# Moving the deep neighbour lists and the biases behind the first blocks of attention in a sparse graph-attention kernel

## The chip, the cores and the metric

The kernel runs on one NeuronCore of a Trainium2 chip. The metric is the time on the device in microseconds (us), lower is better. Five engines work from queues of their own: TensorE (PE, matrix products), VectorE (DVE), ScalarE (ACT), GpSimd (POOL) and SyncE (SP). POOL issues the indirect transfers (gathers and scatters by a list of rows), SP and ACT the plain ones.

## The reference

One layer of graph attention with a residual and a layer norm. There are 16 graphs (b) of 1024 nodes with 512 features in 8 heads of 64, and one adjacency matrix of zeros and ones, shared by all graphs.

```python
q = (x @ Wq + bq).reshape(b, n, H, HD)
k = (x @ Wk + bk).reshape(b, n, H, HD)
v = (x @ Wv + bv).reshape(b, n, H, HD)
scores = einsum('bqhd,bkhd->bhqk', q, k) / sqrt(HD)
scores = scores + (1.0 - adj) * -1e9
out = einsum('bhqk,bkhd->bqhd', softmax(scores), v).reshape(b, n, d)
return layernorm(x + out @ Wo + bo)
```

The entries of adj are drawn with a probability of about 1/256 for the pair on average, weighted so that the first nodes have many neighbours and the last ones few. All is float32.

## The kernel before, in words

Since a node has few neighbours, the kernel gathers keys instead of multiplying all pairs. It ranks the nodes by their number of neighbours, once, and cuts the ranked nodes into 8 tiles of 128. In tile t each node has `OWN[t]` blocks in which one row holds one neighbour of one query (`OWN = (2, 1, 2, 3, 4, 5, 5, 7)`). Tiles 6 and 7 have nodes with more neighbours; what is left over is packed into 1 and 5 further blocks (`BLOCKS`), in which a row holds some query and some key. These need the *deep lists*: which rows, and for which query. `edges(t)` makes them, for t = 7 with up to 80 neighbours and for t = 6 with up to 16.

A *place* is a step of the main loop, numbered n. Places 0 to 543 are the blocks of attention, 34 for each graph (tile 1 is left out, since its queries have one key at most). At place n several blocks are in work at different stages: the gather of keys and values of block n + 8 (`gather`, L984, POOL; 128 rows of 1024 numbers), `products` and `scores` of block n + 4 (qk at L1005 and s at L1009, DVE), the exponential of n + 3 and the weighing of n + 2 (L1019 and L1029, ACT), the sum over a tile's blocks (L1045 on DVE, or for deep blocks L1054 and L1055 on PE). A finished tile is transposed (poT, L1088) and multiplied with Wo (po, L639).

The *fronts* are PE's other work: for each graph the transposes of x (pxT, L606), the products with Wq (pq, L639), and a seven-product scheme for Wk and Wv on a pair of tiles (pair(b, j) takes tiles 2j and 2j+1): products x, pp and z at L763, with PSUM results p6, p7 and p4 in a ring of four buffers named fill (`fill_psum`), and x and z in a bank of their own. DVE and ACT combine them: e (L776), w (L779), g (L782), kv (L786, L791, L795), four sums of x before (L623 to L626), vsum (L701, L704) over the values. When all of a graph's keys and values are written to memory, the mean of its values is made (pm L708, copy L712, written by SP at L713), and `set_up[b]` lets the gathers of that graph start.

The order on each engine is the order in which this loop issues the instructions, and it is written out by hand. `later(k, fn)` puts an action k places on. PE's units are dealt out by credit: each place gets a share of PE time, and units are taken while credit is above 0. The costs are the constants `PRODUCT = 0.86`, `SUM = 0.87`, `TRANSPOSE = 0.44`. Ahead of place 0 lies the lead-in, places -LEAD_IN to -1, with fronts alone: a share of LEAD_SHARE = 3.3 up to place FRONT_BY, then START_SHARE = 2.0. In the first graph's 34 places the share is

```python
goal = fronts_time - (n // NBT + 2 + ahead / NBT) * batch_time
share = (max(0.0, left - goal) + kept * NPAIR * PRODUCT + NS * SUM) / NBT
```

so fronts that the lead-in left over are made up in these places.

Beside the units run generators, each advanced by one `yield` a place: `loads` (weights and biases), `ranks` (the ranking), `checks`, `edges(7)` and `edges(6)`, started at the places in `REST_FROM`, and `bias_setup`, started at `BIAS_AT`. In `edges` the row of adj is gathered (codes, L494), multiplied by the place numbers (L499), and the largest entries are taken out eight at a time, by a maximum (L518) and a removal (L520). For t = 7, sixteen candidates of every 64 columns are taken first (L511 to L513, into found), and ten maxima with nine removals then run on the 256 candidates. From the counts (est, L531) a product over the rows gives each list's start (poff, L534), DVE makes a mask from it (of, L546 and L547), and PE's products (pe, L557) and transposes (pof, L578) turn it into the rows to gather (key_row, L571; query_row, L572) and the sums' matrix. `bias_setup` makes the norm of bk (L351 to L353), columns of the biases (pb, L356 to L363) and bo + bv Wo (pb of L367, L369).

Work buffers come from rings by tag: kvg (8), kv (5), y (6), o (2), pv0 (3), and a new tile waits until the tile that had its buffer is done with.

Of the kernel before, what the change touches and what calls it, by code (L numbers as in the profile page):

```python
# [10 lines left out]
F32 = mybir.dt.float32  # L11
# [6 lines left out]
HEADS = 8  # L18
# [13 lines left out]
KG_BUFS, Q_BUFS, QT_BUFS, PV_BUFS, Y_BUFS = 8, 5, 3, 5, 6  # L32
# [13 lines left out]
EARLY = 13  # L46

FIRST = 11
LEAD_IN = 39
FRONT_BY = -14  # L50
SEGMENT = 64
TOP = 8
ADJ_AT = {-36: (0,), -35: (1, 2), -34: (3, 4), -33: (5,), -32: (6, 7)}
CHECKS_AT = -27
BIAS_AT = -8
REST_FROM = {7: -24, 6: -9}

PRODUCT = 0.86
SUM = 0.87
# [6 lines left out]
P = 128  # L66
# [103 lines left out]
def kernel(  # L170
# [37 lines left out]
    B, N, D = x.shape  # L208
    HD = D // HEADS
    NPAIR = D // P  # L210
# [29 lines left out]
    def broadcast(t, v):  # L240
        nc.scalar.dma_start(t, bass.AP(tensor=v.tensor, offset=v.offset, ap=[[0, P], [1, D]]))
# [4 lines left out]
    with ExitStack() as main:  # L246
        one = main.enter_context(tc.tile_pool(name="one", bufs=1))
        work = main.enter_context(tc.tile_pool(name="work", bufs=1))
# [4 lines left out]
        def fill_psum(name):  # L253
            return psum.tile([P, HALF], F32, tag="fill", name=name, bufs=4)
# [52 lines left out]
        residual = {i: dram.tile([P, D], F32, name=f"residual_{i}") for i in sorted(STORED)}  # L307
        zeros = work.tile([P, D + HEADS], F32, tag="pv0", name="zeros", bufs=3)
        nc.gpsimd.memset(zeros, 0.0)
        bias_rows = work.tile([2 * NPAIR, D + HEADS], F32, tag="pv0", name="bias_rows", bufs=3)[:, 0:P]  # L310
        bv_rows = work.tile([NPAIR, D + HEADS], F32, tag="pv0", name="bv_rows", bufs=3)[:, 0:P]

        def loads():

# [31 lines left out]
        def bias_setup():  # L346
            bk_bc = work.tile([P, D], F32, tag="y", name="bk_bc", bufs=Y_BUFS)
            broadcast(bk_bc, bk)
            yield
            n4 = small.tile([P, NPAIR], F32, name="bk_norms", bufs=1)  # L350
            nc.vector.tensor_tensor(bk_bc, bk_bc, bk_bc, op=OP.mult)  # L351
            nc.vector.tensor_reduce(n4, bk_bc.rearrange("p (h d) -> p h d", d=P), axis=AX.X, op=OP.add)
            nc.vector.tensor_reduce(bk_norm, n4, axis=AX.X, op=OP.max)  # L353
            yield
            pb = fill_psum("pb")
            nc.tensor.transpose(pb[:, 0:2 * NPAIR], bias_rows, ident[:2 * NPAIR, :2 * NPAIR])  # L356
            nc.tensor.transpose(pb[:, 2 * NPAIR:3 * NPAIR], bv_rows, ident[:NPAIR, :NPAIR])
            yield
            nc.vector.tensor_copy(bias_qk, pb[:, 0:2 * NPAIR])
            bv_col = one.tile([P, NPAIR], F32, name="bv_col")  # L360
            nc.vector.tensor_copy(bv_col, pb[:, 2 * NPAIR:3 * NPAIR])
            bvb = work.tile([P, NPAIR, P], F32, tag="y", name="bvb", bufs=Y_BUFS)
            nc.vector.tensor_copy(bvb, bv_col[:, :, None].to_broadcast([P, NPAIR, P]))  # L363
            yield
            pb = fill_psum("pb3")
            for c in range(NPAIR):
                nc.tensor.matmul(pb, bvb[:, c, :], W["o"][:, c, :], start=(c == 0), stop=(c == NPAIR - 1))  # L367
            yield
            nc.vector.tensor_tensor(bo_bc, pb, bo_bc, op=OP.add)  # L369
# [18 lines left out]
        now, plan, rest, urgent, known, waiting, combined = [0], {}, {}, [], [], [], []  # L388
# [9 lines left out]
        def most(t, scratch, copied):  # L398
            nc.vector.tensor_tensor(scratch, ADJ[t], place, op=OP.mult)
            nc.vector.max(out=asked[:, t, 2:], in_=scratch)  # L400
            nc.scalar.activation(copied, ADJ[t], AF.Copy, accum_out=asked[:, t, 1:2])

        def ranks():
# [6 lines left out]
            keys, row = (work.tile([P, N], F32, tag="kv", name=name, bufs=5) for name in ("keys", "key_of"))  # L410
            while now[0] <= max(ADJ_AT):
                for t in ADJ_AT.get(now[0], ()):
                    most(t, keys, row)
# [64 lines left out]
        def checks():  # L478
            for t in range(NT):

                a = ADJ[t]
                nc.scalar.activation(a, a, AF.Square, bias=neg_one, scale=2.0)
                nc.scalar.activation(a, a, AF.Square, bias=neg_one, accum_out=check[:, t:t + 1])
                yield
# [5 lines left out]
        def edges(t):  # L490
            nb, J, K = BLOCKS[t], DEGREE[t], OWN[t]
            tag, bufs = ("kvg", KG_BUFS) if J > 16 else ("kv", 5)
            v = work.tile([P, N], F32, tag=tag, name=f"codes_{t}", bufs=bufs)
# [3 lines left out]
            for _ in range(3):  # L497
                yield
            nc.vector.tensor_tensor(v, v, place, op=OP.mult)  # L499
            of = v[:, 0:nb * P]  # L500
            st = small.tile([P, 4], F32, name="est")
            deg, end, lim, off = (st[:, i:i + 1] for i in range(4))
            kl = small.tile([P, J + 3], F32, tag=f"kl{J}", name=f"kl_{t}", bufs=1)
# [1 line left out]
            if J > SEGMENT:  # L505

                assert J <= N // SEGMENT * 16 <= D
                found = work.tile([P, D], F32, tag="o", name=f"found_{t}", bufs=2)[:, 0:N // SEGMENT * 16]
                for i in range(N // SEGMENT):
                    piece, top = v[:, ts(i, SEGMENT)], found[:, ts(i, 16)]  # L510
                    nc.vector.max(out=top[:, 0:8], in_=piece)  # L511
                    nc.vector.scalar_tensor_tensor(piece, piece, top[:, 7:8], piece, op0=OP.is_lt, op1=OP.mult)
                    nc.vector.max(out=top[:, 8:16], in_=piece)  # L513
                    if i % 4 == 3:
                        yield
                v = found
            for r in range(J // 8):
                nc.vector.max(out=kl[:, ts(r, 8)], in_=v)  # L518
                if r < J // 8 - 1:
                    nc.vector.scalar_tensor_tensor(  # L520
                        v, v, kl[:, r * 8 + 7:r * 8 + 8], v, op0=OP.is_lt, op1=OP.mult
                    )
                    if J <= SEGMENT or r % 3 == 2:
                        yield
            if J > SEGMENT:
# [4 lines left out]

            nc.vector.tensor_scalar(deg, ranked[:, t, 1:2], -float(K), 0.0, op0=OP.add, op1=OP.max)  # L531
            yield
            po = fill_psum(f"poff_{t}")
            nc.tensor.matmul(po[:, 0:1], before, deg, start=True, stop=True)  # L534
            yield
# [6 lines left out]
            nc.vector.scalar_tensor_tensor(  # L542
                check[:, NT + t:NT + t + 1], deg, float(K - J), lim, op0=OP.add, op1=OP.max
            )
            o, span = of, place[:, 0:nb * P]
            nc.vector.tensor_scalar(o, span, off, None, op0=OP.is_gt)  # L546
            nc.vector.scalar_tensor_tensor(o, span, end, o, op0=OP.is_le, op1=OP.mult)  # L547
            yield
            step = min(nb, HALF // (J + 3))
            assert step * J <= D  # L550
# [39 lines left out]
        def load_x(b, t):  # L590
            if b < B:
                if b and not known:
                    waiting.append((b, t))
                    return
                X[b, t] = work.tile([P, D], F32, tag="x", name=f"x_{b}_{t}", bufs=3)
                if b:
                    gather_x(X[b, t], b, t)
                else:
                    nc.sync.dma_start(X[b, t], x[b, ds(t * P, P), :])
# [571 lines left out]
        prep = {}  # L1171
        for t, n in REST_FROM.items():
            prep.setdefault(n, []).append(edges(t))
        prep.setdefault(BIAS_AT, []).append(bias_setup())
        prep.setdefault(CHECKS_AT, []).append(checks())
        preps = [loads(), ranks()]
        prep.setdefault((B - 1) * NBT, []).append(guard())
        prep.setdefault(NBT, []).append(bias_pieces())
        with tc.manual_schedule():
# [6 lines left out]
            batch_time = fronts_time / B  # L1186
            finishing, last_finish, reloads, last_reload = [], -LEAD_IN, 0, 0
            fronts_end = (B - 1) * NBT - 12
            credit = 0.0
            for t in range(3):  # L1190
                load_x(0, t)
            n = -LEAD_IN
            while n < total or plan or rest or urgent or done or finishing or spilled or not guarded:
                now[0] = n
                if n < 0:
                    share = START_SHARE if n > FRONT_BY else LEAD_SHARE if n > -LEAD_IN else TRANSPOSE * 1.5
                elif n >= (LATE + 1) * NBT:
# [110 lines left out]
```

## Time and profile before

| | before |
|---|---|
| median of 3 runs, us | 1927.46 (1924.39 to 1927.83) |
| the profiled execution's own time, us | 1928.59 |
| its span, us | 1926.8 |
| mean granted PE clock | 0.99 |
| PE, DVE, ACT, POOL busy in the span | 96%, 90%, 80%, 71% |
| PE busy from 0 to 40 us | 30.45 us |
| PE busy from 1900 to 1927 us | 11.69 us |
| transfers | 550.85 MB, 286 GB/s |

The span is the time in which the profiler saw the engines at work; the execution's own time also holds what lies around it. Busy shares are averages over stages: the lead-in reaches to about 130 us of the span, and the rest is attention with the fronts of later graphs beside it. A matmul in float32 has two records for each instruction here. A line of the timeline gives start, length, engine, line, operation, output<-inputs, and in brackets how long the engine had been idle and what ended that.

### The profile page before, as it was taken

What the parts mean: (1) busy time and instruction counts of PE and PEld (TensorE: products, weight loads), DVE (VectorE), ACT (ScalarE), POOL (GpSimd) and SP (SyncE); (2) the same over time, 40 slices, a digit from 0 to 9 for tenths busy, and PEclk for the clock granted to TensorE, in tenths of its full rate; (3) what the DMA queues carried; (4) which work ended last, traced back from release to release, by engine and by line L of the source; (5) the groups of instructions that cost most, each with busy time, mean ns of one, the idle gap of its engine ahead of it and who ended that gap; (6) DMA issues with size and microseconds to landing.
All of it is one profiled execution on the core that took longest, in us unless ns stands there. A gap on an engine that the chain in (4) does not pass through costs nothing. (4 is left out here: it accounts for less than half of the span.)

```text
span 1926.8 us, 25037 instructions
## 1 busy us (share of the span) xinstructions
PE 1854.1 (96%) x5247; PEld 898.2 (47%) x5247; DVE 1724.8 (90%) x3494; ACT 1549.6 (80%) x6072; POOL 1368.9 (71%) x1262
## 2 busy tenths in 40 slices
PE   7989999999999999999999999999999989899996
PEld 3444454444544454444544454444544444444443
DVE  6888889899998999899998999899998989798885
ACT  3638779878888888889897888888897988788785
POOL 1336667878787777878778788877787777665785
PEclk9999999999999999999999999999999999999998
DMA  7357788888889898898989898988899898888994
GB/s 273 122 179 243 247 276 265 291 273 290 301 273 314 273 305 299 296 315 296 315 267 323 286 326 288 316 294 297 310 316 325 281 334 301 296 287 283 365 328 167
DMA packets 189313, 550.85 MB, mean 286 GB/s; under 512 B 31359, under 2 KB 31371, under 8 KB 189150
## 3 DMA queue, kind: packets, MB, share of 16 engines
q0 software_dynamic: 133584, 447.59, 69.1%
q1 hardware_dynamic: 52672, 96.04, 13.6%
q10 hardware_dynamic: 2894, 5.52, 0.9%
q14 instruction: 119, 0.97, 0.2%
q8 instruction: 44, 0.72, 0.2%
HBM read 426.56 MB, written 147.18 MB: 298 GB/s over the span
## 5 line engine op out<-in xcount | busy, mean ns | idle before, releaser
L1029 ACT ACTIVATE pv<-kvg,pv 128x64 f32<-128x64 f32 x3544 | 892.1, 338 | 0.0
L984 POOL DMA_INDIRECT kvg<-kv_rows,key_row x544 | 624.6, 1148 | 240.8 <-issue 84.8
L639 PE MATMUL pq<-wq,xT 128*128 128x512 f32 x904 | 422.5, 598 | 0.9 <-ACT mean L712 0.9
L639 PE MATMUL po<-wo,oT 128*128 128x512 f32 x864 | 401.2, 597 | 1.0 <-ACT oT L1092 0.9
L1009 DVE TENSOR_REDUCE s<-qk 128x8 f32<-128x512 f32 x544 | 369.5, 679 | 7.5
L1005 DVE TENSOR_TENSOR qk<-qt,kvg 128x512 f32<-128x512 f32 x448 | 306.5, 684 | 37.4 <-DMA kvg<-kv_rows,key_row 37.0
L639 PEld LDWEIGHTS pq<-wq,xT 128*128 128x128 f32 x904 | 169.1, 192 | 193.4 <-issue 179.4
L639 PEld LDWEIGHTS po<-wo,oT 128*128 128x128 f32 x864 | 162.9, 191 | 182.9 <-issue 169.4
L763 PE MATMUL x<-b,xT 128*128 128x512 f32 x504 | 238.1, 595 | 0.0
L763 PE MATMUL pp<-t,s 128*128 128x512 f32 x504 | 237.4, 593 | 0.0
L1045 DVE TENSOR_TENSOR pv<-pv,pv 128x520 f32<-128x520 f32 x336 | 232.7, 692 | 0.9 <-ACT pv L1029 0.9
L1019 ACT ACTIVATE pv<-s,absent 128x8 f32<-128x8 f32 x448 | 130.2, 292 | 84.7 <-DVE s L1009 79.3
L817 POOL DMA_INDIRECT x<-in_x_dram,asked_row x120 | 134.2, 1118 | 76.7 <-PE pxT L606 34.6
L893 POOL DMA_INDIRECT out_dram<-y,asked_row x128 | 146.8, 1147 | 40.8 <-issue 19.3
L685 POOL DMA_INDIRECT kv_rows<-kv,asked_row x120 | 135.9, 1132 | 33.8 <-issue 22.9
L649 ACT ACTIVATE sq_k<-kv 128x128 f32<-128x128 f32 x512 | 150.6, 299 | 7.8 <-DVE kv L786 7.8
L763 PEld LDWEIGHTS x<-b,xT 128*128 128x128 f32 x504 | 95.2, 191 | 114.9 <-issue 109.2
L763 PEld LDWEIGHTS pp<-t,s 128*128 128x128 f32 x504 | 94.3, 190 | 110.6 <-issue 102.6
L954 POOL DMA_INDIRECT qg<-q_rows,query_row x96 | 108.1, 1126 | 31.2 <-issue 25.7
L763 PE MATMUL z<-b,s 128*128 128x512 f32 x252 | 118.8, 594 | 1.0 <-DVE kv L791 0.9
L763 PE MATMUL z<-t,s 128*128 128x512 f32 x252 | 119.6, 597 | 0.0
L763 PE MATMUL pp<-t,xT 128*128 128x512 f32 x252 | 118.4, 592 | 0.0
(208 smaller groups left out, 2666.3 us busy)
## 6 DMA issues: line engine op xcount, KB each, us to landing
q_rows<-q SPq DMA_DIRECT2D x113, 256.0 KB
qt<-q_rows SPq DMA_DIRECT2D x105, 256.0 KB
residual<-x SPq DMA_DIRECT2D x42, 256.0 KB
y<-residual SPq DMA_DIRECT2D x42, 256.0 KB
kvg<-kv_rows,key_row POOLq DMA_INDIRECT x544, 5.9
spill<-oT SPq DMA_DIRECT2D x20, 256.0 KB
oTs<-spill SPq DMA_DIRECT2D x20, 256.0 KB
adj<-in_adj_dram POOLq DMA_DIRECT2D x8, 512.0 KB, 13.4
```

The lines of the kernel that those rows point to most:

```text
L639: nc.tensor.matmul(p, lhs(c), w[:, c, :], start=(c == 0), stop=(c == NPAIR - 1))
L649: nc.scalar.activation(sq, s[:, ts(h, P)], AF.Square, scale=scale, accum_out=sums[:, h:h + 1])
L685: later(2, lambda: nc.gpsimd.indirect_dma_start(out=kv_views[b % ROWS][tt[i]], out_offset=bass.IndirectOffsetOnAxis(ap=asked_row[:, tt[i]: ...
L763: nc.tensor.matmul(R[bank], l[:, ts(c, P)], right[:, c, :], start=(first and c == 0), stop=(c == 1), skip_group_check=True,)
L817: nc.gpsimd.indirect_dma_start(out=y, out_offset=None, in_=x_rows, in_offset=bass.IndirectOffsetOnAxis(ap=asked_row[:, t:t + 1], axis=0), ...
L893: nc.gpsimd.indirect_dma_start(out=out_rows[b, t], out_offset=bass.IndirectOffsetOnAxis(ap=asked_row[:, t:t + 1], axis=0), in_=y, in_offse ...
L984: nc.gpsimd.indirect_dma_start(out=KG[n], out_offset=None, in_=kv_rows[b % ROWS], in_offset=bass.IndirectOffsetOnAxis(ap=key_row[:, g:g + ...
L1005: nc.vector.tensor_tensor(QK[n], q, KG[n][:, 0:D], op=OP.mult)
L1009: nc.vector.tensor_reduce(S[n], QK.pop(n).rearrange("p (h d) -> p h d", d=HD), axis=AX.X, op=OP.add)
L1019: nc.scalar.activation(PV[n][:, D:], S.pop(n), AF.Exp, bias=bias)
L1029: nc.scalar.activation(pv[:, ts(h, HD)], v[:, ds(D + h * HD, HD)], AF.Copy, scale=pv[:, D + h:D + h + 1])
L1045: nc.vector.tensor_tensor(PV[b, t], PV[b, t], pv, op=OP.add)
```

## The change

The lead-in has 35 places instead of 39; the places with a share of 3.3 are as many as before, those with 2.0 four fewer. What is tied to a place in the lead-in moves along by four. Three things move further. The ten rounds on found for tile 7 wait for place -3 (`REST_ON`); they were at places -16 to -13. `edges(6)` starts at place -1 instead of -9, and `bias_setup` at 0 instead of -8. A few generators get one more `yield`, so that steps lie a place further apart. The mask of tile 7 gets a buffer of its own from the ring kvg, and that of tile 6 a fixed one, instead of lying in codes; found and the rows of the biases come from the ring y instead of o and pv0.

```diff
--- before.py
+++ after.py
@@ -46,14 +46,15 @@
 EARLY = 13
 
 FIRST = 11
-LEAD_IN = 39
-FRONT_BY = -14
+LEAD_IN = 35
+FRONT_BY = -10
 SEGMENT = 64
 TOP = 8
-ADJ_AT = {-36: (0,), -35: (1, 2), -34: (3, 4), -33: (5,), -32: (6, 7)}
-CHECKS_AT = -27
-BIAS_AT = -8
-REST_FROM = {7: -24, 6: -9}
+ADJ_AT = {-32: (0,), -31: (1, 2), -30: (3, 4), -29: (5,), -28: (6, 7)}
+CHECKS_AT = -23
+BIAS_AT = 0
+REST_FROM = {7: -20, 6: -1}
+REST_ON = -3
 
 PRODUCT = 0.86
 SUM = 0.87
@@ -307,8 +308,8 @@
         residual = {i: dram.tile([P, D], F32, name=f"residual_{i}") for i in sorted(STORED)}
         zeros = work.tile([P, D + HEADS], F32, tag="pv0", name="zeros", bufs=3)
         nc.gpsimd.memset(zeros, 0.0)
-        bias_rows = work.tile([2 * NPAIR, D + HEADS], F32, tag="pv0", name="bias_rows", bufs=3)[:, 0:P]
-        bv_rows = work.tile([NPAIR, D + HEADS], F32, tag="pv0", name="bv_rows", bufs=3)[:, 0:P]
+        bias_rows = work.tile([2 * NPAIR, D], F32, tag="y", name="bias_rows", bufs=Y_BUFS)[:, 0:P]
+        bv_rows = work.tile([NPAIR, D], F32, tag="y", name="bv_rows", bufs=Y_BUFS)[:, 0:P]
 
         def loads():
 
@@ -347,6 +348,7 @@
             bk_bc = work.tile([P, D], F32, tag="y", name="bk_bc", bufs=Y_BUFS)
             broadcast(bk_bc, bk)
             yield
+            yield
             n4 = small.tile([P, NPAIR], F32, name="bk_norms", bufs=1)
             nc.vector.tensor_tensor(bk_bc, bk_bc, bk_bc, op=OP.mult)
             nc.vector.tensor_reduce(n4, bk_bc.rearrange("p (h d) -> p h d", d=P), axis=AX.X, op=OP.add)
@@ -361,6 +363,7 @@
             nc.vector.tensor_copy(bv_col, pb[:, 2 * NPAIR:3 * NPAIR])
             bvb = work.tile([P, NPAIR, P], F32, tag="y", name="bvb", bufs=Y_BUFS)
             nc.vector.tensor_copy(bvb, bv_col[:, :, None].to_broadcast([P, NPAIR, P]))
+            yield
             yield
             pb = fill_psum("pb3")
             for c in range(NPAIR):
@@ -497,7 +500,6 @@
             for _ in range(3):
                 yield
             nc.vector.tensor_tensor(v, v, place, op=OP.mult)
-            of = v[:, 0:nb * P]
             st = small.tile([P, 4], F32, name="est")
             deg, end, lim, off = (st[:, i:i + 1] for i in range(4))
             kl = small.tile([P, J + 3], F32, tag=f"kl{J}", name=f"kl_{t}", bufs=1)
@@ -505,7 +507,7 @@
             if J > SEGMENT:
 
                 assert J <= N // SEGMENT * 16 <= D
-                found = work.tile([P, D], F32, tag="o", name=f"found_{t}", bufs=2)[:, 0:N // SEGMENT * 16]
+                found = work.tile([P, D], F32, tag="y", name=f"found_{t}", bufs=Y_BUFS)[:, 0:N // SEGMENT * 16]
                 for i in range(N // SEGMENT):
                     piece, top = v[:, ts(i, SEGMENT)], found[:, ts(i, 16)]
                     nc.vector.max(out=top[:, 0:8], in_=piece)
@@ -514,6 +516,8 @@
                     if i % 4 == 3:
                         yield
                 v = found
+                while now[0] < REST_ON:
+                    yield
             for r in range(J // 8):
                 nc.vector.max(out=kl[:, ts(r, 8)], in_=v)
                 if r < J // 8 - 1:
@@ -530,6 +534,7 @@
 
             nc.vector.tensor_scalar(deg, ranked[:, t, 1:2], -float(K), 0.0, op0=OP.add, op1=OP.max)
             yield
+            yield
             po = fill_psum(f"poff_{t}")
             nc.tensor.matmul(po[:, 0:1], before, deg, start=True, stop=True)
             yield
@@ -542,9 +547,14 @@
             nc.vector.scalar_tensor_tensor(
                 check[:, NT + t:NT + t + 1], deg, float(K - J), lim, op0=OP.add, op1=OP.max
             )
+            if nb > 1:
+                of = work.tile([P, 2 * D], F32, tag="kvg", name=f"of_{t}", bufs=KG_BUFS)[:, 0:nb * P]
+            else:
+                of = one.tile([P, P], F32, name=f"of_{t}")
             o, span = of, place[:, 0:nb * P]
             nc.vector.tensor_scalar(o, span, off, None, op0=OP.is_gt)
             nc.vector.scalar_tensor_tensor(o, span, end, o, op0=OP.is_le, op1=OP.mult)
+            yield
             yield
             step = min(nb, HALF // (J + 3))
             assert step * J <= D
```

## The prediction

> **What bounds the kernel now.** First the page's busy shares and slices, to see which engine sets the pace and where it doesn't.
>
> ```profile
> span 1926.8 us, 25037 instructions
> PE 1854.1 (96%) x5247; PEld 898.2 (47%) x5247; DVE 1724.8 (90%) x3494; ACT 1549.6 (80%) x6072; POOL 1368.9 (71%) x1262
> ...
> PE   7989999999999999999999999999999989899996
> ...
> DVE  6888889899998999899998999899998989798885
> ...
> PEclk9999999999999999999999999999999999999998
> ```
>
> TensorE (PE) is busy for 1854.1 of 1926.8 us. A digit of 9 hides small gaps, so I looked at stretches of the time behind the lead-in. The columns are PE, weight loads, DVE, ACT and POOL, busy us and instructions, then the granted clock, DMA share and GB/s.
>
> ```profile
> 80.00:120.00 40.00, 36.01 (x98) 16.45 (x97) 33.11 (x101) 9.94 (x42) 6.00 (x7) 0.91 0.34 117
> 120.00:160.00 40.00, 37.65 (x106) 17.37 (x104) 36.75 (x83) 22.58 (x97) 25.42 (x24) 1.00 0.79 248
> 160.00:200.00 40.00, 40.00 (x116) 19.19 (x115) 33.23 (x60) 32.53 (x134) 26.24 (x24) 1.00 0.78 247
> ```
>
> From 160 us on PE has no gap, so time lost on PE before that isn't given back. Between 80 and 160 it loses time and clock. The waits of PE from 101 to 160 us name two places:
>
> ```profile
> PE poff L534 <- DVE est L531: 4.0, 1, 4.0
> PE pb L367 <- DVE bvb L363: 2.2, 1, 2.2
> ```
>
> Both belong to the work that the change moves. PE's timeline shows what the first costs:
>
> ```profile
> 101.04 2.74 PE L639 MATMUL pq<-wq,xT 128*128 128x512 f32 x6
> 107.77 0.59 PE L534 MATMUL poff<-est,before 128*128 128x1 f32 x2 [3.99 <-DVE est L531]
> 108.22 2.06 PE L639 MATMUL pq<-wq,xT 128*128 128x512 f32 x2
> 110.20 1.86 PE L708 MATMUL pm<-vsum,mean 128*1 128x512 f32 x2
> 112.00 3.05 PE L763 MATMUL x<-b,xT 128*128 128x512 f32 x4
> ```
>
> A 128x512 product has two records, start to start 0.86 us elsewhere in the trace. Behind the gap pq takes 1.98, pm 1.80 and the two products of x 2.89 instead of 1.72: 3.2 us lost to the clock, besides the gap. I add up all PE work from 101.04 to 168.50 us (the start of pp<-t,xT of the pair of tiles 4 and 5, batch 1) at full-clock spacing: 56.5 us. The stretch has 67.5, so **10.9 us are lost there now**. DVE's timeline shows what occupies DVE ahead of the gap, a round of the deep list in 0.97 us:
>
> ```profile
> 98.97 0.42 DVE L518 MAX8 kl<-found 128x8 f32<-128x256 f32 x1
> 99.42 0.48 DVE L520 SCALAR_TENSOR_TENSOR found<-found,kl 128x256 f32<-128x256 f32 x1
> 99.94 0.43 DVE L518 MAX8 kl<-found 128x8 f32<-128x256 f32 x1
> ```
>
> [...] a wait of only 1.89 us at 369.66 is also followed by matmuls at double length for some 3 us (1.8 us lost), while the 2.2 us of pb is not, so shorter gaps can cost too. [...]
>
> **The change part by part.**
>
> *Four places fewer.* The places dropped are four of START_SHARE 2.0. No unit of PE work goes: by the kernel's own unit costs (PRODUCT 0.86 and so on) the lead-in issues 109.4 us of fronts before and 101.6 after, places 0 to 33 124.8 and 132.6, both 234.2 together. The share of places 0 to 33 rises from 3.80 to 4.03. PE is the full engine there, so I price this at 0. All engines have as many instructions as before, no DMA is added, and 1926.8 us of span stands.
>
> *The waits taken out.* The 10 maxima and 9 removals (9.2 us of DVE) no longer stand ahead of est, vsum and w, and bvb no longer behind them with pb waiting: the 10.9 us can go. What covered the rounds was DVE time in the lead-in that PE didn't need; after the change DVE is idle there, since REST_ON holds the rounds until place -3.
>
> *The waits put in: first.* Block 0's product stands at place -4, but set_up of batch 0 now comes at place -6 (before -10), and the first gather at -5 (before -8). So the mean's chain is on the path. PE: pq's four units from 101.04 end at 104.48, pm at 105.34. From pm's end at 112.06 to the gather's start is 2.65 us in the lines of ACT and POOL below, and the median landing of such a gather between 100 and 170 us is 5.2.
>
> ```profile
> 112.11 0.58 ACT L712 COPY mean<-pm 1x512 f32<-1x512 f32 x1 [7.66 <-PE pm L708]
> ```
>
> ```profile
> 114.71 1.02 POOL L984 DMA_INDIRECT kvg<-kv_rows,key_row  x1 [8.00 <-DMA kv_rows<-mean]
> ```
>
> ```profile
> kvg<-kv_rows,key_row POOLq DMA_INDIRECT x16, 5.2
> ```
>
> DVE's first qk then starts at 105.34 + 2.65 + 5.2 = 113.2. Behind it in DVE's queue stands kv_1_1<-z, which frees z and lets PE's last product of the pair start. PE reaches that at 104.48 + 8.61 (pm 0.86, x, pp, z, pp at 1.72 each, transposes 0.87) = 113.1; DVE is through at 113.2 + 1.32 (qk, s) + 0.65 = 115.2. **Wait 2.1 us.**
>
> *Second.* PE then does 12.5 us (z, x, pp, x, pp at 1.72, pq 3.44, one transpose 0.44) up to pxT of tile 5 at 127.7. That takes the fill bank of pp6, which is released by w_1_1 on DVE (the built program has that wait). From 113.2 DVE has: five qk and s 6.6; kv_1_1 twice 1.25; four sums s 1.45; nine rounds 8.7; kv_1_0, vsum, w and the norm 1.9. That is 19.9, so w_1_1 ends at 133.1. **Wait 5.4 us**, over the length that halved the clock: another 3.2.
>
> *Third.* From w_1_1 to q_1_4 DVE has 27.5 us, some 10 of them moved here (codes of tile 6 with its two maxima 4.8, the biases' 2.2, masks and offsets 2.1, the last round 1.2). PE has 22.0 and the 3.2 of half clock up to pxT of tile 7, which needs q_1_4, so it waits 2.3 more; with query_row ahead of pb3 and the copy of oT behind an exponential, about **3.2 us** in small pieces. POOL's queue takes six gathers at place -5 and codes_6 at place -1; with 1.3 us per issue they land 5 us ahead of their products, price 0. ACT, busy 9.9 of 40 us in that stretch, gets nothing more than its blocks; price 0.
>
> Sum: 2.1 + 5.4 + 3.2 + 3.2 = 13.9, and of the two groups of 2 us one followed by half clock, 1.8: 15.7 lost against 10.9. **Net +4.8 us, taken as +5.** The profiled execution took 1928.59 us (1.79 outside its span), so 1933.6 for its like; it lies 1.1 above the median of the three runs, 1927.46, hence 1932.5.
>
> Bounds of what the trace doesn't show: the gather lands in 4.1 to 6.0 us (-1.1 to +0.8); half clock behind small gaps 0 to 3.6 (-1.8 to +1.8)[...]. The waits of sums on DVE later (24.5 us over the run) shift with the order, either way by some 4.
>
> **The rivals.** (1) *Even*: the new waits weigh what the old did. If the long gap costs no clock, 12.5 against 10.9; with an early landing and luck later 0, so 1927.5. (2) *Faster*: DVE's added work fits beside PE, and poff, bvb and the half clock behind them vanish: -9.6, so 1918. For it speaks that DVE is 83% busy from 160 to 200 us; against it that places -4 to -1 give PE 2.0 us each, and DVE some 5 with three rounds. It decides if w_1_1 ends by 125.6 + 2.1 = 127.7, that is if DVE's 19.9 us were 14.5. (3) *Much slower*: each wait halves the clock and the ring of kvg, from which the mask of tile 7 takes a buffer for four places, holds gathers too: +12, so 1939. (4) The change doing nothing to the order is excluded by the built program, whose lists stand behind blocks 0 to 14.
>
> **How the numbers follow.** Mine 0.52 (0.45 over +0.2%, 0.07 within), even 0.25 (0.22 within, 0.03 slower), faster 0.09, much slower 0.14. A measurement of this kernel tells about 0.2% (3.9 us) from no change. Faster 0.09, same 0.29, slower 0.62. Two in ten outside gives 1923 to 1942: the lower end is -4.5, nearly all bounds on their good side; the upper is past the third rival.
>
> **What would show it.** Right: the wait of poff on est gone; DVE waiting for the first kvg near 113 us; PE waiting for kv at L791 some 2 us and at a transpose of x at L606 some 5 us with a clock below 0.95 behind it; pp<-t,xT of tiles 4 and 5 starting 3 to 5 us later than 168.50. Wrong: no wait over 3 us on PE between 110 and 170 us, or that product earlier than 168.5; then the faster case holds. A median that differs while that product stands where the sum has it would put the cause in later batches.

## The result and the profile after

| | before | after |
|---|---|---|
| median, us | 1930.92 (11 runs, 1924.39 to 1935.45) | 1936.93 (11 runs, 1935.22 to 1940.67) |
| profiled execution, us | 1928.59 | 1936.43 |
| span, us | 1926.8 | 1934.6 |

The changed kernel takes 1.0039 of the time before, interval 1.0025 to 1.0053: slower by 6.0 us in the medians, 7.5 by the ratio (which is not the quotient of the two medians). The forecast was +5. Three things from the page answer to those shown of before: busy shares, slices of PE and DVE, and the granted clock.

```profile
span 1934.6 us, 25035 instructions
PE 1859.2 (96%) x5240; PEld 901.3 (47%) x5247; DVE 1726.1 (89%) x3494; ACT 1550.4 (80%) x6072; POOL 1369.3 (71%) x1262
...
PE   8989999899999999999999999999999989799996
...
DVE  6879789899998999999998999899998979898885
...
PEclk9999999999999999999999999999999999999998
```

No engine has more work: DVE 1726.1 against 1724.8, ACT and POOL within 1 us. PE is busy 5.1 us longer (1859.2 for 1854.1) with no more products to do, so part of the loss is slower products and the rest is waits. The page can't show where. The three stretches, with the columns of before (PE, weight loads, DVE, ACT, POOL, clock, DMA share, GB/s):

```profile
80.00:120.00 40.00, 38.10 (x101) 17.13 (x100) 26.86 (x79) 14.90 (x64) 11.49 (x11) 1.00 0.46 159
120.00:160.00 40.00, 34.06 (x94) 16.24 (x93) 38.65 (x81) 21.75 (x92) 21.49 (x20) 0.91 0.71 237
160.00:200.00 40.00, 38.46 (x114) 18.63 (x115) 36.73 (x86) 28.93 (x119) 20.58 (x20) 1.00 0.62 201
```

The first stretch is better than before (PE 38.10 for 36.01, clock 1.00 for 0.91), with DVE at 26.86 us instead of 33.11: the rounds have left it. The second is worse by more than the first gained (PE 34.06 for 37.65, clock 0.91 for 1.00), with DVE full at 38.65 of 40. The waits of PE from 101 to 180 us, each as total, count and longest:

```profile
PE pxT L616 <- DVE w L789: 5.0, 1, 5.0
PE z L773 <- DVE kv L801: 1.9, 1, 1.9
PE pxT L616 <- ACT oT L1102: 1.8, 1, 1.8
PE pp L773 <- DVE w L789: 0.5, 1, 0.5
```

The waits of poff on est and of pb on bvb, 4.0 and 2.2 us before, are gone. PE's timeline gives what follows the two long waits:

```profile
112.50 1.88 PE L773 MATMUL pp<-t,xT 128*128 128x512 f32 x4
116.28 1.99 PE L773 MATMUL z<-b,s 128*128 128x512 f32 x4 [1.90 <-DVE kv L801]
118.10 1.88 PE L773 MATMUL x<-b,xT 128*128 128x512 f32 x4
...
134.03 1.11 PE L616 MATMUL pxT<-ident,x 128*128 128x128 f32 x4 [5.03 <-DVE w L789]
134.94 3.62 PE L773 MATMUL z<-t,s 128*128 128x512 f32 x4
138.35 4.15 PE L649 MATMUL pq<-wq,xT 128*128 128x512 f32 x8
142.34 1.88 PE L773 MATMUL pp<-t,xT 128*128 128x512 f32 x4
...
172.34 1.88 PE L773 MATMUL pp<-t,xT 128*128 128x512 f32 x4
```

Start to start, z behind the first wait takes 1.82 us: nearly full clock. Behind the second the transposes take 0.91 instead of 0.44, z 3.41 instead of 1.72, pq 3.99 instead of 3.44: 2.7 us lost, and the granted clock from 134.03 to 138.40 is 0.50, against 1.00 from 116.28 to 118.10. The last line is the product that the prediction watches, at 172.34 for 168.50. DVE's timeline says what held it:

```profile
110.11 0.69 DVE L792 TENSOR_TENSOR g<-pp,w 128x512 f32<-128x512 f32 x1 [3.80 <-PE pp L773]
114.21 0.69 DVE L1015 TENSOR_TENSOR qk<-qt,kvg 128x512 f32<-128x512 f32 x1 [3.41 <-DMA kvg<-kv_rows,key_row]
...
115.54 0.68 DVE L801 TENSOR_TENSOR kv<-z,g 128x512 f32<-128x512 f32 x1
...
133.29 0.68 DVE L789 TENSOR_TENSOR w<-pp,e 128x512 f32<-128x512 f32 x1
```

Between 100.8 and 114.2 us DVE stands still for 11.2 us in four gaps (1.36, 2.67, 3.80, 3.41; the last two are in the lines). From 114.21 it has no gap, and w, on which PE stands for 5 us, comes out at 133.97. The work was moved from a place where DVE now idles to one where it is behind.

### The profile page after: what moved, and what is told of

Its sections match the earlier page's. It is cut to its first block, busy times and chain, and to the rows that moved or that the text cites. A ratio compares the mean times of both kernels' runs of the same rounds, so it can differ in the third digit from the quotient of the medians.

```text
span 1934.6 us, 25035 instructions
## 1 busy us (share of the span) xinstructions
PE 1859.2 (96%) x5240; PEld 901.3 (47%) x5247; DVE 1726.1 (89%) x3494; ACT 1550.4 (80%) x6072; POOL 1369.3 (71%) x1262
## 5 line engine op out<-in xcount | busy, mean ns | idle before, releaser
L1015 DVE TENSOR_TENSOR qk<-qt,kvg 128x512 f32<-128x512 f32 x448 | 307.3, 686 | 41.6 <-DMA kvg<-kv_rows,key_row 41.5
L695 POOL DMA_INDIRECT kv_rows<-kv,asked_row x120 | 139.4, 1161 | 36.8 <-issue 24.7
```

Of the source, the lines that this page charges most:

```text
L695: later(2, lambda: nc.gpsimd.indirect_dma_start(out=kv_views[b % ROWS][tt[i]], out_offset=bass.IndirectOffsetOnAxis(ap=asked_row[:, tt[i]: ...
L1015: nc.vector.tensor_tensor(QK[n], q, KG[n][:, 0:D], op=OP.mult)
```

## The experiments

Ratios are to the kernel before, run on the same chip; its median there was 1929.46 for the first four experiments, 1930.65 for the next four and 1927.32 for the last four. Each run has two marks on PE. "The product" is pp<-t,xT of tiles 4 and 5 of batch 1: 168.50 before, 172.34 after. Where an edit carries PE work past it, it misleads, so I also give "the second mean", pm of the second graph, with the same work ahead of it in all kernels: 204.68 before, 208.11 after. A second profile of each gives 169.16 and 205.3 (before), 172.02 and 207.8 (after), so a mark repeats to some 0.7 us. (With a third profile of after, below, the second mean averages 205.0 before and 208.0 after.)

### The rounds four places earlier

```diff
-REST_ON = -3
+REST_ON = -7
```

> The changed kernel with REST_ON = -7 instead of -3: the rounds of the deep list run four places earlier, in the stretch from 102 to 114 us in which the changed kernel's DVE waits for PE and for the first gather (1.4, 2.7, 3.8 and 3.4 us). Theory D (DVE's sum): from the first qk (114.2) to q_1_4 (161.3) PE is led by DVE's queue, 47 us of work; nine rounds less is 8.7 us less, so PE's product pp<-t,xT of tiles 4 and 5 starts 7 to 9 us earlier than 172.3, the wait at w is under 1 us, and the time is 7 to 9 us below the changed kernel, 1 to 3 below the kernel before. Rival P (the single wait at w and the half clock behind it): 5.0 + 3.2 = 8.2 less, hardly different here. Rival L (the loss comes later, from the order of later batches): less than 3 us gained.

1929.40 us, ratio 0.9992 (0.998 to 1.0004). The product comes at 164.82 and the second mean at 200.48, 7.5 and 7.6 us earlier than in the changed kernel. PE's waits from 98 to 180 us:

```profile
PE pxT L616 <- ACT oT L1102: 2.5, 1, 2.5
PE z L773 <- DVE kv L801: 1.6, 1, 1.6
PE pp L773 <- DVE s L635: 0.7, 1, 0.7
```

The 5 us on w are gone and with them the half clock: from 116 to 165 us the products of 128x512 start 0.86 to 0.92 us apart where PE doesn't wait. Where the rounds stand is worth the whole loss, 1.0039 against 0.9992. It is not the whole story: the second mean is 4.2 us ahead of before, and the time only level with it.

### The rounds three places later

```diff
-REST_ON = -3
+REST_ON = 0
```

> The changed kernel with REST_ON = 0: the rounds stand behind w_1_1 and no longer ahead of it, but still ahead of q_1_4. Theory D: DVE's work from the first qk to q_1_4 is the same but for some 2.8 us of offsets and masks that fall behind it; the wait at w shrinks below 1 us, yet others take its place (g, q and kv of the next tiles), and the time is 1 to 4 us below the changed kernel. Rival P: wait and half clock gone, 8 us below the changed kernel. Rival L: no difference.

1936.40 us, ratio 1.0030 (1.0021 to 1.0040); the second mean at 207.52, 0.6 earlier than after (the product, at 170.19, has 1.5 us of the mask's products behind it that stood ahead). If the wait on w were the cause by itself, taking the rounds from ahead of w should have paid as in the run before. The wait goes to the next thing that DVE owes, with the same half clock behind it (pp takes 3.56 us to the next start instead of 1.72); PE's timeline:

```profile
138.93 1.88 PE L773 MATMUL x<-b,xT 128*128 128x512 f32 x4
145.06 3.63 PE L773 MATMUL pp<-t,s 128*128 128x512 f32 x4 [4.25 <-DVE s L635]
```

So it is DVE's running sum from the first qk on, not the order of two instructions. Time alone would not tell this run from rival L's "no difference" (1.0030 and 1.0039, intervals that overlap); the moved wait does, and rival P is out.

### No hold at all

```diff
-REST_ON = -3
+REST_ON = -30
```

> The changed kernel with REST_ON = -30, so that the rounds aren't held and run at places -12 to -9 as in the kernel before; the second list, the biases and 35 places stay as changed. Theory D: vsum and pm wait behind the rounds as they did before (pm near 109 instead of 105.4), with half clock behind that wait, 7 to 8 us lost there, but DVE is free of 9 rounds later and catches up by q_1_4: 3 to 6 us below the changed kernel, about level with the kernel before. Rival P: the wait at w goes and one of the same kind at pm comes, so 0 to 2 us below the changed kernel. Rival L: no difference from the changed kernel.

1932.26 us, ratio 1.0023 (1.0009 to 1.0036); the product at 168.80, the second mean at 204.45, as in before. The rounds now stand so early that vsum is late, and PE waits for it:

```profile
PE pm L718 <- DVE vsum L714: 4.4, 1, 4.4
```

Too early costs as well: it is the loss of before with another instruction behind the rounds. The expected size against the changed kernel holds by the ratios, but the run is not level with before: the 0.23% above it are not in the early stretch.

### The kernel before with four places fewer

```diff
-LEAD_IN = 39
-FRONT_BY = -14
+LEAD_IN = 35
+FRONT_BY = -10
...
-BIAS_AT = -8
-REST_FROM = {7: -24, 6: -9}
+BIAS_AT = -4
+REST_FROM = {7: -20, 6: -5}
```

ADJ_AT and CHECKS_AT move by four as well.

> The kernel before with the four places fewer alone: LEAD_IN 35, FRONT_BY -10, and all that is tied to a place in the lead-in four places on (second list at -5, biases at -4); rounds, buffers and yields as before. Theory D: the wait at poff stays (4.0 us and half clock), the wait for the first gather is hidden behind it, w waits some 2 us behind the biases and codes; 10 to 12 us lost in the stretch against 10.9 before, so the time within 3 us of the kernel before. A theory that the shorter lead-in by itself costs (the first gather at place -5): 4 to 6 us above the kernel before. That it gains: 8 us (four places of 2.0) below it.

1932.15 us, ratio 1.0009 (0.9998 to 1.0019), so no proven difference. The early waits are those of before (3.9 on est, 1.3 on bvb), and the marks are 167.98 and 203.31, not later than in before.

### The moves with 39 places

```diff
-LEAD_IN = 35
-FRONT_BY = -10
+LEAD_IN = 39
+FRONT_BY = -14
...
-REST_FROM = {7: -20, 6: -1}
+REST_FROM = {7: -24, 6: -1}
```

This is the changed kernel with the long lead-in (ADJ_AT, CHECKS_AT as before, REST_ON still -3).

> The changed kernel with the 39 places of before (LEAD_IN 39, FRONT_BY -14, ADJ_AT, CHECKS_AT and the first deep list's start as before): rounds from place -3, second list at -1, biases at 0 as changed. Theory D (DVE's sum): the first gather has long landed when its qk comes; PE meets one wait of some 6 us at z for kv_1_3 behind nine rounds and six blocks, with half clock behind it, but DVE's sum up to q_1_4 ends near 155 instead of 161: 4 to 7 us below the changed kernel, within 3 us of the kernel before. Theory R (the rounds behind attention cost the same whatever the lead-in): within 2 us of the changed kernel.

1930.97 us, ratio 1.0004 (0.9992 to 1.0017). PE has one long wait from 98 to 180 us, of the kind forecast, and half clock behind it: z and x take 6.51 us to the next product instead of 3.44.

```profile
140.49 3.78 PE L773 MATMUL z<-b,s 128*128 128x512 f32 x4 [6.51 <-DVE kv L801]
...
147.00 1.88 PE L773 MATMUL pp<-t,s 128*128 128x512 f32 x4
```

The product stands at 164.20, but the biases' product (L370) and the mask's, some 5 us of PE work, have gone behind it. The second mean, 206.04, is 1.4 later than before and 2.1 earlier than after. So together with the moves the four places do cost some 2 us early, though alone they cost none.

### The same with the rounds where DVE idles

```diff
-REST_ON = -3
+REST_ON = -11
```

on top of the edit before.

> As the last one, with REST_ON = -11: the rounds stand behind the first w of the second graph, where DVE waits for PE, and the second list and the biases behind the first blocks, with 39 places. Theory D: no wait on PE over 3 us between 100 and 160 us, no half clock; some 5 us lost against 10.9 before: 4 to 7 us below the kernel before. Theory S (the later batches lose some 5 us in every kernel with 35 places, seen in the four runs so far between the second and the sixth graph's mean, and not with 39): the gain up to the second graph's mean is kept to the end. If the later loss is rather a lucky profile of before: the gain up to there is 6 to 9 us and shrinks by some 4.

**1923.07 us (8 runs), ratio 0.9955 (0.9934 to 0.9975): faster than both kernels.** The second mean comes at 199.15, 5.5 us earlier than before (the product at 158.98, with the biases' product behind it). The same three stretches:

```profile
80.00:120.00 40.00, 40.00 (x106) 17.95 (x106) 34.90 (x106) 13.13 (x55) 11.37 (x11) 1.00 0.44 146
120.00:160.00 40.00, 37.21 (x117) 18.39 (x116) 37.79 (x70) 29.14 (x122) 27.12 (x26) 1.00 0.85 291
160.00:200.00 40.00, 40.00 (x109) 18.20 (x108) 35.25 (x80) 28.05 (x118) 23.01 (x23) 1.00 0.72 230
```

PE is full up to 120 us (40.00 of 40), and the granted clock is 1.00 in all three stretches. DVE's busy time to 120 us goes from 26.86 (after) to 34.90: the rounds fill its gaps from 103 to 115 us, between two instructions that wait for PE anyway. PE's longest wait from 98 to 180 us is 1.3. Here the second deep list and the biases lie behind the first blocks, as in the change; only the rounds don't. The gain is a little above the 4 to 7 us expected. That it is kept to the end is not shown by the trace: its execution took 1927.34, 4.3 above the median, and its last graph's mean (1775.7) lies between those of the two profiles of before (1775.1 and 1779.1).

### Both kernels again

No edit; a profile each.

> The kernel before once more, unchanged, for a second profile. Theory S: the graphs' means come within 2 us of the first profile up to the last. Otherwise (the first profile was lucky in graphs 3 to 5): they come 3 to 5 us later from the sixth graph on, with the second graph's within 1 us.

> The changed kernel once more, unchanged, for a second profile. Theory D and S: the second graph's mean near 208, 3 us behind before; the sixth graph's near 675, 8 us behind. If the spread between executions is as large as the later loss: the sixth graph's mean anywhere from 670 to 677.

Before: 1932.51 us, waits of 3.9 on est and 2.2 on bvb. After: 1930.85 us, waits of 5.0 on w, 1.8 on kv, 1.8 on oT. In these pairs the waits repeat to 0.1 us, and in the further profiles with the same first graph (below) to 0.4. The whole does not: this execution of after is 6 us below the median of the first measurement. Its second mean is at 207.8, as expected, but the sixth at 670.7 and not near 675 (675.1 in the first profile), so the case holds that executions of one kernel spread as much as the later loss. Before keeps within 1 us up to the sixth mean (665.7 for 666.7), and its last mean is 4.0 later. A single profile says where early time goes, not which kernel is faster.

### The planner's credit at the end of the first graph

The four places were priced at 0, yet the kernels with 35 places came out later than their early gains. In the built programs the PE order from the mean of the second graph on is one and the same in all kernels with 35 places, and another one in those with 39; the credit left at place 34 is -1.21 after and -0.97 before, and the same 0.24 lies between them at place 0 already (-0.44 and -0.20). The next kernels swap only that, at the start of the second graph. The orders of PE, DVE and ACT from the third graph on are then those of the other kernel.

```diff
+                if n == NBT:
+                    credit += 0.24
                 credit += paced(share, n) if n >= 0 else share
```

in the changed kernel; -0.24 in the kernel before; and 0.24 with the rounds at -7.

> The changed kernel with 0.24 us added to the credit of PE's units at place 34, so that from the third graph on all three engines issue in the order of the kernel before; the first 34 places stay as changed. Theory S (the shorter lead-in shifts the phase of the credit, and the order that follows from it costs some 3 us in the later graphs): 2 to 4 us below the changed kernel, ratio to before 1.0010 to 1.0025. Theory N (the order of the later graphs is worth nothing; all of the 6 us are lost before 170 us and the rest is spread of the executions): within 1.5 us of the changed kernel, ratio 1.003 to 1.004.

> The kernel before with 0.24 us taken from the credit at place 34, so that from the third graph on it issues in the order of the changed kernel; the first 34 places as before. Theory S: 2 to 4 us above the kernel before, ratio 1.0010 to 1.0020. Theory N: within 1.5 us of it.

> The changed kernel with REST_ON = -7 and the order of before from the third graph on. Theory S: 2 to 4 us below the run with REST_ON = -7 alone (ratio 0.9992), so ratio 0.997 to 0.9985. Theory N: ratio 0.9985 to 1.000.

> The changed kernel, unchanged, timed on the chip of the three others. Both theories: ratio 1.0025 to 1.0045, and PE's product pp<-t,xT of tiles 4 and 5 near 172.2 in the profile.

| | median, us | ratio |
|---|---|---|
| changed | 1937.16 | 1.0043 (1.0030 to 1.0056) |
| changed, old order later | 1931.28 | 1.0021 (1.0013 to 1.0028) |
| before, new order later | 1935.05 | 1.0042 (1.0027 to 1.0058) |
| rounds at -7, old order later | 1926.22 | 0.9996 (0.9987 to 1.0005) |
| rounds at -7 (with the first experiments, on another chip) | 1929.40 | 0.9992 (0.998 to 1.0004) |

The new order costs the kernel before 0.42% with its early stretch untouched, and taking it from the changed kernel wins back 5.9 us in the medians (0.22% in the ratios). With the rounds at -7 no difference shows, where theory S had 2 to 4 us; theory S's size fits the first pair by the ratio and is half of what the second shows. So the price of the new order is real in two pairs on one chip. That it differs between kernels is likely but less sure, because the third pair was timed on two chips and its intervals leave room for some 2 us. The changed kernel with the old order also isolates the early stretch: 1.0021, 4.0 us, are left of the loss.

Where it lies, the traces tell in part. From the mean of the fourth graph to that of the sixth (434.1 to 666.7 us before) the eight profiles with the new order take 1.9 to 7.5 us longer than the mean of the two of before; the four others with the old order are within 0.5. The waits of PE from 430 to 675 us in the changed kernel:

```profile
PE poT L1098 <- DVE g L792: 3.0, 1, 3.0
PE po L649 <- ACT xT L620: 1.6, 1, 1.6
```

and in the changed kernel with the old order later:

```profile
PE poT L1098 <- DVE g L792: 1.2, 1, 1.2
```

The wait of po on ACT's copy of xT (1.2 to 1.6 us) is in all eight profiles with the new order and in none of the six with the old. The wait on g is in all, mostly longer with the new order (1.1 to 4.4 against 1.0 to 2.3). In the changed kernel the granted clock behind it is 0.66 from 624.43 to 629.02, and three products of pq take 3.68 us to the next start instead of 2.58:

```profile
624.43 1.12 PE L1098 MATMUL poT<-ident,o 128*128 128x128 f32 x4 [2.97 <-DVE g L792]
625.34 3.85 PE L649 MATMUL pq<-wq,xT 128*128 128x512 f32 x6
629.02 1.88 PE L773 MATMUL pp<-t,xT 128*128 128x512 f32 x4
```

Later some of it comes back: from the sixth mean to the eleventh these eight gain 0.7 to 3.9 us on before, three of the four others up to 1.9, and the fastest kernel loses 1.9. From the second mean to the last, the eight lie between 0.8 ahead and 5.0 behind the mean of the two profiles of before, and the six with the old order (those two among them) between 1.7 ahead and 4.5 behind. So single traces don't carry the price; it rests on the medians. The before kernel with the new order, for one, was profiled in an execution of 1932.14, below its median, and little of its +8 us is in that trace.

The traces do say what the executions spread by. Between the second mean and the last, the two profiles of before differ by 3.3 us: 0.6 of it lies in PE's waits and nearly all the rest, by an estimate from the start-to-start times, in slower products. By neither measure do the two orders stand apart over that whole stretch: the waits sum to 37.5 to 41.5 us with the new order and 35.7 to 39.7 with the old, slower products cost an estimated 11 to 18 and 13 to 19. That all of this is half clock is not shown: in the first profiles the granted clock is 0.50 for 20.5 us of the stretch before and 27.3 after, which costs at most half of it, 10.2 and 13.7. So where the price of the new order lies stays open.

## Why the prediction was right

Direction and size hold: +5 forecast, +6.0 measured, inside the range. The time itself is 4.4 us above the 1932.5 forecast, mostly because the median of before moved from 1927.46 to 1930.92 with more runs. The mechanism that the prediction named, a wait on DVE behind the first blocks, is shown. But the steps say that part of the size is luck.

| step | forecast | profile after |
|---|---|---|
| first qk on DVE | 113.2 | 114.21 |
| wait of z on kv_1_1 | 2.1 | 1.9 |
| w_1_1 done | 133.1 | 133.97 |
| wait of pxT on w_1_1 | 5.4 | 5.0 |
| half clock behind it | 3.2 | 2.7 |
| the rest up to the product | 3.2 | 4.7 |
| half clock behind a group of 2 us | 1.8 | 0 |
| lost up to the product | 15.7 | 14.3 |

- **The waits put in.** The stretch from pq (101.90) to the product (172.34) has 70.4 us. Less the 56.5 of PE work, of which 0.4 (products of the second list) now stand behind the mark, 14.3 are lost. DVE's queue explains it nearly to the term: PE came to this stretch 0.9 us later than in the first profile of before (its second has pq at 101.85, so this is spread), and qk and w are later by that. The gather's start after the mean's product was 2.7 us (2.65 forecast), its landing 5.0 (5.2). The rest is the wait on oT of 1.8, that on the last w of 0.5, and pieces below half a us.
- **The waits taken out.** est, bvb and their 10.9 us are gone, as forecast (before, DVE came to est only at 107.56 us, behind the last maximum at 106.41). So the early stretch costs 14.3 - 10.9 = 3.4 us net in this profile, not 4.8; the second mean is 3.0 later on all profiles, and the run with the old order later has 4.0 us by its ratio. The missing term is the half clock behind one of the 2 us groups: here it came neither behind the 1.90 us nor behind the 1.83 on oT. In the changed kernel timed again it did, behind the very same 1.83 us. First this profile, then that one:

```profile
161.41 1.29 PE L616 MATMUL pxT<-ident,x 128*128 128x128 f32 x8 [1.83 <-ACT oT L1102]
162.53 1.88 PE L773 MATMUL z<-t,s 128*128 128x512 f32 x4
...
160.19 1.29 PE L616 MATMUL pxT<-ident,x 128*128 128x128 f32 x8 [1.83 <-ACT oT L1102]
161.32 3.33 PE L773 MATMUL z<-t,s 128*128 128x512 f32 x4
164.44 2.18 PE L649 MATMUL pq<-wq,xT 128*128 128x512 f32 x4
```

There z takes 3.12 us to the next start instead of 1.72, and up to the product 15.2 us are lost, close to the 15.7 forecast. So the term of 1.8 is a matter of chance: with the same first graph and the same wait it came in one of these two profiles.

- **The length of the half clock.** In the traces the granted clock is 0.50 for 6.8 us at the 3.99 us gap of before (107.4 to 114.2) and for 6.8 at the 5.03 us gap of after (132.6 to 139.4), and for 3.4 at the 1.89 us gap of before (370.2 to 373.6). It falls 0.4 us before PE starts again in the first and 1.4 before in the second, and 3.2 and 2.7 us are lost. That the long wait would cost as much as the 3.99 us had, 3.2, was the author's estimate from that one gap.
- **Four places fewer, at 0: wrong.** Early the price holds (neither mark later with nothing else changed). What it left out is the credit of 0.24 us that the shorter lead-in hands on, which gives the later graphs another order. In the two comparisons with the rounds at their own place this cost 5.9 and about 8 us, with the rounds at -7 nothing measurable. The prediction let later waits shift by some 4 either way and took none. Its premise that PE has no gap from 160 us on is shown for 160 to 200 only: its own wait at 369.66 is later, and both profiles of before have over 38 us of PE waits between the second mean and the last. Its last sentence, that a median off the sum would put the cause in later batches, fits the later timing: there the changed kernel's median is 9.8 us above that of before (1937.16 and 1927.32), and 3.4 + 5.9 = 9.3 account for it (by the ratios 8.3, for 3.4 + 4.2 = 7.6). The first measurement's 6.0 has a before of 1930.92. So a term that comes by chance, 1.8, stood in the sum where a larger one was missing.
- **The zero prices of POOL and ACT** held up to the product: DVE waits for a gather only ahead of the first qk (3.4 us), and no wait of PE on ACT there is over 1.8 us. The line for ACT was misread, though: its 9.9 of 40 us belong to 80 to 120 us, and in the stretch meant, 120 to 160, the line shows 22.58.
- **The rivals.** *Faster* fell on the point given for it: DVE's sum was 19.8 us (114.21 to 133.97), not 14.5. Yet much of its -9.6 us is there to be had: with 39 places and the rounds in DVE's gaps the median falls by 7.6, of which 5.5 are seen by the second mean. The covering time in the lead-in existed, and the change held the rounds out of it. *Even* needed no half clock. *Much slower* needed it behind each wait, and the ring of kvg holding gathers up; DVE waited for none but the first.

## What to carry to other kernels

Deferred work was cheap here only where its engine idled: with 39 places the median is 1923.07 us with the rounds in DVE's gaps and 1930.97 with them behind the first blocks. Look for the gaps of that engine between two instructions that wait for another one (here four gaps of 11.2 us together), and put the work there, neither behind (5 us wait) nor ahead (4.4 us wait) of what the full engine waits for. Where a planner carries a remainder from one stage to the next, an edit that adds and removes no work can still reorder all later stages: compare the built orders, and test the remainder by itself.

## What the runs showed that was not expected

- In these traces the length of a gap does not tell whether the clock falls. Gaps of 3.99 (before) and 5.03 us lost a further 3.2 and 2.7; one of 2.97 lost 1.6 (0.5 on the transposes, 1.1 on pq), one of 2.20 (changed kernel timed again, at 621.79 us) lost 1.7; 1.90 lost 0.1 and 1.83 at most 0.3 in the first profile of after (granted clock 1.00 behind both), while 1.89 lost 1.8 in before (0.50 from 370.2 to 373.6 us), and the same 1.83 lost 1.4 on z alone in the changed kernel timed again. A wait of 2.52 us on oT likewise lost nothing in the run with the rounds at -7, while one of 2.26 on oT with REST_ON = 0 lost 1.7 (eight transposes take 1.73 us instead of 0.87, z 2.59 instead of 1.72). On these numbers a price per gap is a likelihood, not a sum. Six gaps between 100 and 170 us were each followed by slower products: 3.88 us (four places fewer, 1.7 lost), 3.99 (before, 3.2), 4.25 (REST_ON = 0, 1.8 on pp), 4.41 (no hold, 2.7), 5.03 (after, 2.7) and 6.51 (39 places, 3.1); of the shorter ones, some.
- Executions of the kernel before lie from 1923.40 to 1939.50 us over the runs, while the second mean of two profiles of it differs by 0.7. In these two the difference is made later in the run, by the estimate above mostly in slower products.
